# A graph layer's gathers: all but 28 tiles of rows by GpSimd, none picked column by column

## The chip, the core and the metric

The kernel runs on one core of a Trainium2 chip. The core has five engines with a program each: TensorE (PE, matmuls), VectorE (DVE), ScalarE (ACT), GpSimd (POOL) and SyncE (SP, which here issues DMAs). They run side by side and wait for one another through semaphores. The metric is the device time of one execution in microseconds (us), as the median of several runs.

## The reference

One layer of a graph network over 12500 nodes with 128 features and 412500 edges, followed by a layer norm. The edges are sorted by their target `dst`, and `src` is random. Cut to what matters:

```python
f0 = x0 @ W1_0e / sqrt(MUL)                      # node features, x0 = x[:, :32]
f1 = einsum('nui,uw->nwi', x1, W1_1o) / sqrt(MUL)  # x1 = x[:, 32:] as 32 vectors of 3
e0, e1 = feat0[edge_src], feat1[edge_src]        # one row of 128 numbers per edge
h = gelu(gelu(edge_scalar_attr @ W_mlp1 / sqrt(8)) @ W_mlp2 / sqrt(64))
w00, w01, w10, w11 = h @ Wp_00, h @ Wp_01, h @ Wp_10, h @ Wp_11
mid0, mid1 = ...                                 # products of w, e and edge_attr, per edge
n0, n1 = segment_sum(mid0, edge_dst), segment_sum(mid1, edge_dst)
y = cos(MIX) * self + sin(MIX) * (n0 @ W2_0e, n1 @ W2_1o)
out = layernorm(x + y)
```

The step `feat[edge_src]` is the gather that this change is about: 412500 rows of 128 float32 numbers, 512 bytes each, from a table of 12500 rows.

## The kernel before

The edges are cut into runs of 512, 806 of them, the last with 340 edges. A run has four tiles (called columns in the code, q = 0 to 3) of 128 edges, one edge to a partition. Four runs make a chunk, 202 in all. For every run the kernel needs the features of its sources in a buffer `G` of 128 x 4 x 128 numbers. There are LEAD = 19 such buffers.

Before the runs start, a first phase of 25 groups of 512 nodes loads x, transposes it into `xT` (it stays in SBUF, a node to a column), multiplies it by the weights `wf` and stores the result in DRAM as `table`. The first RAW = 18 runs do not wait for the table: their rows of x itself are gathered (indices in `idx_raw`), transposed (`turn_rows`, L569 and L571) and multiplied by `wf` (`features`, L577 and L579), and the result stands in a buffer `ft`; their buffer G is free once it is transposed. All later runs gather finished features from `table`.

Then one long loop goes over the runs s. Its order is written out by hand and holds for PE, ACT, DVE and SP. In iteration s it

- calls `gather(s + 18)`, which takes the next buffer G, the one that run s - 1 had, and so has to wait until that run's reader is done;
- issues some loads of edge data, and 16-row parts of an aided tile (below);
- makes the edge weights of runs ahead on PE (`weights`, L560), and once per chunk the two layers of the small network (`mlp1`, L527 and L531, `mlp2`, L542 and L547);
- sums the messages of run s - 1 on PE (`segments`, L631 and L633), with an address per tile read from a register;
- multiplies weights and features of run s on DVE (`messages`, one product at L602 and two at L606), which frees the buffer G;
- adds a finished chunk into an accumulator (`add`, L646), and about every 32 runs ends a group of nodes (`norm` and what follows it: PE at L662 and L665, ACT at L670, DVE at L678, the store of `out` by SP at L257 and L259).

A tile of rows gets into G in one of three ways:

1. *GpSimd gathers it*: one indirect DMA of 128 rows, L220, with the node numbers in `idx` (transposed by PE for 128 runs at a time).
2. *SyncE copies it* (`aid`, L203 and L207): in every AID = 14th run from run 36 on, the last tile's 128 rows are 128 DMAs of 512 bytes, with node numbers loaded into registers. They are issued in eight sets of 16 rows (ROWS), spread over STEPS = 12 runs, the first 16 runs (AID_LEAD) ahead of use. There are 55 such tiles, 7040 copies.
3. *VectorE or ScalarE picks it* (`pick_nodes` and `pick`): the tile's 128 node numbers, turned into addresses at L163, are loaded into registers (L176), and each node's column is copied out of `xT` into a buffer `gt`, 128 x 1 at a time (DVE at L188, ACT at L190). `picked_rows` then multiplies the finished `gt` by `wf` on PE (L196) and ACT copies the result into G (L197). DVE picks tile q = 2, ACT tile q = 1. The table `SLOTS` says how many columns each picks: DVE 8, 12 and 12 after the three products of a run, ACT 24 or 28 in a run, so a tile takes four or five runs. From the run COL_FROM on this gives 197 tiles of DVE and 157 of ACT.

What the three leave over follows from these lines of `gather`:

```python
            if q == Q - 1 and s in aided or any(q == COL_Q[e] and (e, s) in pick_of for e in picked):
                continue
            rows = idx_raw[:, s, q:q + 1] if s < raw_runs else idx[b][:, q, c:c + 1]
            nc.gpsimd.indirect_dma_start(
```

Of 806 x 4 tiles one lies past the last edge; 3223 - 55 - 354 = 2814 are gathered by GpSimd.

Of the kernel before, what the change touches and what calls it, by code (L numbers as in the profile page):

```python
# [15 lines left out]
ACT = mybir.EngineType.Activation  # L16
DVE = mybir.EngineType.DVE
# [4 lines left out]
P = 128  # L22
# [20 lines left out]
RAW = 18  # L43
MARGIN = 64
ACC = 768
AID = 14
ROWS = 16
AID_FROM = 36
AID_LEAD = 16
STEPS = 12  # L50
SLOTS = {DVE: [(8, 12, 12)], ACT: [(24,), (28,), (24,), (28,), (24,)]}
COL_Q = {DVE: Q - 2, ACT: Q - 3}
COL_FROM = {DVE: 11, ACT: 16}
LNB = 2


# [1 line left out]
def gnn_kernel(ctx: ExitStack, tc: tile.TileContext, x, src, dst, ea4, ea8, w1_0, w1_1, wm1, wm2,  # L58
# [26 lines left out]
    def sub(ap, offset, dims):  # L85
        return bass.AP(tensor=ap.tensor, offset=ap.offset + offset, ap=dims)
# [24 lines left out]
    G, GT, Y = {}, {}, {}  # L111
    aided = range(AID_FROM, NS - 1, AID)

    slot_at = {}
    for e, cycle in SLOTS.items():
        slot_at[e], n = {}, 0
        for s in range(COL_FROM[e], NS):
            for slot, k in enumerate(cycle[(s - COL_FROM[e]) % len(cycle)]):
                slot_at[e][s, slot] = (n, n + k)
                n += k  # L120

    picked = {}
    for e in SLOTS:
        picked[e] = []
# [6 lines left out]
    pick_of = {(e, s): i for e, g in picked.items() for i, s in enumerate(g)}  # L131
    assert AID_FROM >= raw_runs and AID_LEAD < LEAD and P % ROWS == 0 and STEPS <= AID
    assert all(raw_runs <= g[0] and 0 < len(g) <= 3 * P for g in picked.values())
# [5 lines left out]
    def aid_load():  # L139


        nc.sync.dma_start(aid_at, sub(src, AID_FROM * SB + (Q - 1) * P, [[AID * SB, len(aided)], [1, P]]))
        for e, g in picked.items():
            n = sum(sum(run) for run in SLOTS[e])
            cycle, ahead = n // math.gcd(n, P), P // math.gcd(n, P) * len(SLOTS[e])
            assert all(z - a == ahead for a, z in zip(g, g[cycle:]))
# [15 lines left out]
        for rows in pick_tiles:  # L162
            nc.vector.tensor_scalar(rows, rows, 4.0, float(x_at), op0=OP.mult, op1=OP.add)  # L163

    picking = {e: [] for e in picked}

    def pick_nodes(e, s, slot):

        a, z = slot_at[e].get((s, slot), (0, 0))
        z = min(z, P * len(picked[e]))  # L170
        while a < z:
            i, r0 = divmod(a, P)
            r1 = min(P, r0 + z - a)
            if r0 == 0:
                GT[e, i] = wk.tile([P, P], F32, name=f"gt{list(picked).index(e)}", bufs=3)
            _, r = nc.values_load_multi_w_load_instructions(  # L176
                pick_rows[e, i][:, r0:r1], engines=[e], min_val=x_at, max_val=x_at + 4 * (N - 1),
                skip_runtime_bounds_check_because="addresses of columns")
            for k in range(r1 - r0):
                at = r[k].with_bounds(guaranteed_mod_val=0, out_of_modulus=4)  # L180
                picking[e].append((GT[e, i][:, r0 + k:r0 + k + 1], x_bytes[:, bass.ds(at, 4)].bitcast(F32)))
            a += r1 - r0
# [661 lines left out]
    with tc.manual_schedule(engines={PE, ACT, DVE, SP}):  # L844
# [46 lines left out]
        A["now"] = A["next"]  # L891
        clearing = []
        pick_nodes(ACT, 0, 0)
        for s in range(NCH * CH + CH):
            c, k = divmod(s, CH)
# [10 lines left out]
            for t in range(P // ROWS):  # L906
                a = s + AID_LEAD - t * STEPS // (P // ROWS)
                if a in aided:
# [19 lines left out]
            if k > 1 and c + 2 < NCH:  # L928
                pick(ACT, P)
                (mlp1 if k == 2 else mlp2)(c + 2)  # L930
                if k == 3 and c + 3 == NCH:
                    nc.scalar.activation(spent, ones, AF.Sqrt)
            pick(ACT, P)
            pick_nodes(ACT, s + 1, 0)
            if s + 1 < raw_runs:
                turn_rows(s + 1)
            if s < NS:
                for part in range(3):
                    messages(s, part)
                    pick_nodes(DVE, s, part)  # L940
                    pick(DVE, P)
# [53 lines left out]
```

## Time and profile before

| | before |
|---|---|
| runs, us | 3772.66, 3779.92, 3783.14 (median 3779.92) |
| profiled execution, us | 3778.12 |
| its span, first to last instruction, us | 3776.3 |
| mean granted clock of TensorE | 0.903 |
| gathers by GpSimd (from x, from the table) | 72 + 2742 |
| row copies by SyncE | 7040 |
| columns picked by VectorE, by ScalarE | 25216, 20096 |
| DMA, mean over the span | 64 GB/s |

The profile is one execution. Its page gives busy times by engine, the chain of work that ended last followed back from the end, and groups of instructions by line. A group's row reads: line, engine, operation, output and input, shapes and count, then busy time in us and the mean of one in ns, then the idle time of that engine just before these instructions and what ended most of it. "issue" there means that the engine waited for nothing that the profile shows. A row of the timeline reads: start in us, duration in us, engine, line, operation and tiles, and in brackets the idle time ahead of it. The duration of a gather is the time that GpSimd is busy with it, not the time until its rows have landed.

### The profile page before, as it was taken

The numbers are of one execution on the slowest core, as the hardware profiler recorded it, in microseconds if no ns is written. First come the engines' busy times: TensorE is split into PE (matmuls) and PEld (weight loads), VectorE is DVE, ScalarE is ACT, GpSimd is POOL, SyncE is SP. The second block draws the span as 40 slices with busy tenths as digits, with TensorE's granted clock in tenths as the row PEclk, the third lists the DMA queues.
The fourth block names the chain that finished last, engine by engine and source line by source line (L and its number), as shares of the span: only waits on it lengthen the run. The fifth ranks groups of instructions, "written<-read, shape, count | busy, mean of one in ns | idle before, by whom it ended". The sixth has DMA issues, their size and how long they took to land.

```text
span 3776.3 us, 140497 instructions
## 1 busy us (share of the span) xinstructions
PE 3310.0 (88%) x28568; PEld 2904.3 (77%) x28568; DVE 3188.6 (84%) x28801; ACT 2613.7 (69%) x21733; POOL 2678.4 (71%) x2820
## 2 busy tenths in 40 slices
PE   5888898998898999899898898898898889989888
PEld 4777777777777887787777777777787777878777
DVE  3488898888888899888889888888888888988887
ACT  2377677777676777667767677777777777777775
POOL 7667776777777777677777677677777777767770
PEclk8998898998898899889899899999889889889898
DMA  8223222323222223222233223222322222222220
GB/s 203 48 51 67 60 60 62 63 57 70 61 57 63 63 60 68 61 56 63 61 63 68 58 62 63 58 63 62 68 59 60 60 64 62 61 64 62 58 62 14
DMA packets 579364, 240.07 MB, mean 64 GB/s; under 512 B 483702, under 2 KB 528654, under 8 KB 578510
## 3 DMA queue, kind: packets, MB, share of 16 engines
q0 software_dynamic: 90048, 184.60, 19.1%
q1 hardware_dynamic: 467692, 39.95, 8.7%
q10 hardware_dynamic: 20770, 6.47, 0.7%
q8 instruction: 252, 4.13, 0.4%
q14 instruction: 602, 4.93, 0.4%
HBM read 217.98 MB, written 12.80 MB: 61 GB/s over the span
## 4 chain that ended last, share of the span: by engine, by line
DVE 52%; PE 15%; issue 10%; DVEq 7%; SPq 6%; ACT 5%; DMA 3%; POOL 1%; ACTq 0%; POOLq 0%
DVE gt L188 30%; DVE M L606 14%; DVEq L176 7%; SPq L207 4%; DVE M L602 4%; ACT gt L190 3%; PE sums L631 3%; PE sums L633 3%; PE h L665 2%; PE w L560 2%; PE h L527 2%; DMA G<-table,idx 1%; SPq L203 1%; DVE acc L646 1%; POOL G L220 1%
## 5 line engine op out<-in xcount | busy, mean ns | idle before, releaser
L220 POOL DMA_INDIRECT G<-table,idx x2742 | 2609.0, 952 | 988.0 <-issue 759.6
L190 ACT ACTIVATE gt<-xT 128x1 f32 x20096 | 1970.7, 189 | 318.1 <-issue 316.6
L188 DVE COPY gt<-xT 128x1 f32 x25216 | 1758.2, 144 | 306.8 <-issue 210.3
L633 PE MATMUL sums<-own,M 128*128 128x96 f32 x6446 | 1347.3, 293 | 38.0 <-DVE M L606 37.9
L631 PE MATMUL sums<-own,M 128*128 128x96 f32 x6446 | 1379.6, 298 | 0.0
L631 PEld LDWEIGHTS sums<-own,M 128*128 128x128 f32 x6446 | 1078.5, 207 | 84.4 <-issue 18.7
L633 PEld LDWEIGHTS sums<-own,M 128*128 128x128 f32 x6446 | 1069.5, 208 | 51.6 <-DVE M L606 50.8
L560 PE MATMUL w<-wpb,h 64*128 64x128 f32 x6448 | 722.8, 311 | 269.2 <-DVE M L606 268.2
L560 PEld LDWEIGHTS w<-wpb,h 64*128 64x128 f32 x6448 | 545.6, 201 | 426.9 <-DVE M L606 308.9
L606 DVE TENSOR_TENSOR M<-w,G 128x384 f32<-128x384 f32 x1576 | 861.5, 547 | 0.0
L531 ACT ACTIVATE h<-h 128x512 f32<-128x512 f32 x404 | 216.7, 587 | 226.2 <-PE h L527 215.6
L527 PE MATMUL h<-eT,w1b 64*128 64x128 f32 x3232 | 328.9, 349 | 10.1 <-ACT G L197 7.3
L602 DVE TENSOR_TENSOR M<-w,G 128x256 f32<-128x256 f32 x788 | 321.9, 409 | 10.0 <-ACT G L197 4.0
L527 PEld LDWEIGHTS h<-eT,w1b 64*128 64x128 f32 x3232 | 281.1, 246 | 41.2 <-issue 16.8
L542 PE MATMUL h<-h,w2b 64*64 64x256 f32 x3232 | 248.1, 392 | 3.1 <-ACT h L531 2.6
L197 ACT ACTIVATE G<-h 128x128 f32<-128x128 f32 x354 | 96.2, 272 | 209.0 <-PE h L196 186.8
L547 ACT ACTIVATE h<-h 128x512 f32<-128x512 f32 x404 | 214.4, 580 | 29.5 <-PE h L542 24.3
L196 PE MATMUL h<-wf,gt 128*128 128x128 f32 x708 | 152.0, 298 | 17.1 <-ACT eT L520 14.9
L542 PEld LDWEIGHTS h<-h,w2b 64*64 64x64 f32 x3232 | 117.0, 133 | 62.7 <-ACT G L197 9.9
L595 DVE TENSOR_TENSOR own<-oh,e 128x512 f32<-128x512 f32 x202 | 140.3, 695 | 7.1
L196 PEld LDWEIGHTS h<-wf,gt 128*128 128x128 f32 x708 | 114.0, 203 | 25.2 <-ACT eT L520 23.5
L646 DVE TENSOR_TENSOR acc<-sums,acc 128x384 f32 x202 | 111.1, 550 | 8.5 <-issue 6.2
(112 smaller groups left out, 1232.9 us busy)
## 6 DMA issues: line engine op xcount, KB each, us to landing
G<-table SPq DMA_DIRECT2D x7040, 0.5 KB
G<-table,idx POOLq DMA_INDIRECT x2742
e<-in_edge_attr SPq DMA_DIRECT2D x201, 64.0 KB
xt<-in_x SPq DMA_DIRECT2D x24, 256.0 KB
table<-ft ACTq DMA_DIRECT2D x24, 256.0 KB
xt<-in_edge_attr SPq DMA_DIRECT2D x24, 256.0 KB
out<-y SPq DMA_DIRECT2D x24, 256.0 KB
xt<-in_dst SPq DMA_DIRECT2D x5, 256.0 KB
```

Source lines behind the costliest of these rows:

```text
L176: _, r = nc.values_load_multi_w_load_instructions(pick_rows[e, i][:, r0:r1], engines=[e], min_val=x_at, max_val=x_at + 4 * (N - 1), skip_r ...
L188: nc.vector.tensor_copy(to, col)
L190: nc.scalar.activation(to, col, AF.Copy)
L196: nc.tensor.matmul(pt, GT.pop((e, i)), wf, start=True, stop=True)
L220: nc.gpsimd.indirect_dma_start(out=G[s][:, q, :], out_offset=None, in_=x if s < raw_runs else table, in_offset=bass.IndirectOffsetOnAxis(a ...
L527: nc.tensor.matmul(p1[h][:, j // 2, j % 2, :], w1b[rows, j, :], eT[c][rows, :], start=True, stop=True)
L542: nc.tensor.matmul(p2[r][k * HID:(k + 1) * HID, h * n:(h + 1) * n], w2b[rows, :], H1[c][h][rows, k * n:(k + 1) * n], start=True, stop=True)
L560: nc.tensor.matmul(WP[i][:, q, :], H2[c][q % 2][rows, k, q // 2, :], wpb[rows, :], start=True, stop=True)
L602: nc.vector.tensor_tensor(M[s][:, :, :, :MUL], w[:, :, :2 * MUL].rearrange("p q (a u) -> p q a u", a=2), g[:, :, None, :MUL].to_broadcast( ...
L606: nc.vector.tensor_tensor(M[s][:, :, j, MUL:].rearrange("p q (i u) -> p q i u", i=3), w[:, :, None, (2 + j) * MUL:(3 + j) * MUL].to_broadc ...
L631: nc.tensor.matmul(flat[:, bass.ds(at, 4 * FIRST_HALF)].bitcast(F32), M[s][:, q, 0, :], own[:, 3 * WIDE:], start=False, stop=False)
L633: nc.tensor.matmul(sb[:, 1:, bass.ds(at, 4 * WIDE)].bitcast(F32), M[s][:, q, 1, :], own[:, :3 * WIDE].rearrange("p (a j) -> p a j", a=3), ...
```

## The change

The table of picked columns becomes empty, the aided run is every 28th, and its row copies are spread over 16 runs. The rest of the diff lets the loop run with an empty table; `COL_FROM` has no effect then.

```diff
-AID = 14
+AID = 28
 ROWS = 16
 AID_FROM = 36
 AID_LEAD = 16
-STEPS = 12
-SLOTS = {DVE: [(8, 12, 12)], ACT: [(24,), (28,), (24,), (28,), (24,)]}
+STEPS = 16
+SLOTS = {}
 COL_Q = {DVE: Q - 2, ACT: Q - 3}
-COL_FROM = {DVE: 11, ACT: 16}
+COL_FROM = {DVE: 7, ACT: 16}
...
-    picking = {e: [] for e in picked}
+    picking = {e: [] for e in (DVE, ACT)}
...
-        a, z = slot_at[e].get((s, slot), (0, 0))
-        z = min(z, P * len(picked[e]))
+        a, z = slot_at[e].get((s, slot), (0, 0)) if e in picked else (0, 0)
+        z = min(z, P * len(picked.get(e, ())))
```

With the table empty, `picked` has no entries: L163, L176, L188, L190, L196 and L197 are not in the program, and no pick tables are loaded. The aided tiles are 28 (runs 36, 64 and so on to 792), 3584 row copies. GpSimd's list has 3195 gathers. With 16 steps the eight sets of an aided tile stand 16, 14, 12 and so on to 2 runs ahead of its use; with 12 steps the last stood 6 ahead.

## The prediction

> **What bounds the kernel now.** First the page: busy time by engine, and the chain of waits by engine.
>
> ```profile
> PE 3310.0 (88%) x28568; PEld 2904.3 (77%) x28568; DVE 3188.6 (84%) x28801; ACT 2613.7 (69%) x21733; POOL 2678.4 (71%) x2820
> DVE 52%; PE 15%; issue 10%; DVEq 7%; SPq 6%; ACT 5%; DMA 3%; POOL 1%; ACTq 0%; POOLq 0%
> ```
>
> By these two lines VectorE (DVE) and TensorE (PE) set the pace, GpSimd (POOL) has 29% to spare and stands in 1% of the chain. So work taken from VectorE and given to GpSimd looks like a gain. The next view, the groups of instructions, contradicts the spare time.
>
> ```profile
> L220 POOL DMA_INDIRECT G<-table,idx x2742 | 2609.0, 952 | 988.0 <-issue 759.6
> L190 ACT ACTIVATE gt<-xT 128x1 f32 x20096 | 1970.7, 189 | 318.1 <-issue 316.6
> L188 DVE COPY gt<-xT 128x1 f32 x25216 | 1758.2, 144 | 306.8 <-issue 210.3
> ...
> L197 ACT ACTIVATE G<-h 128x128 f32<-128x128 f32 x354 | 96.2, 272 | 209.0 <-PE h L196 186.8
> ...
> L196 PE MATMUL h<-wf,gt 128*128 128x128 f32 x708 | 152.0, 298 | 17.1 <-ACT eT L520 14.9
> ```
>
> Of GpSimd's 988 us idle ahead of its gathers, 759.6 are put down to "issue", that is, to nothing else on the chip. The timeline of GpSimd alone shows what that is. Its columns: start, duration, instruction, and in brackets the idle time before it.
>
> ```profile
> 5.00 0.94 POOL L220 DMA_INDIRECT G<-in_x,idx_raw  x1 [0.30 <-issue]
> ...
> 52.43 0.94 POOL L220 DMA_INDIRECT G<-in_x,idx_raw  x1 [0.30 <-issue]
> ...
> 2000.14 0.94 POOL L220 DMA_INDIRECT G<-table,idx  x1 [0.30 <-DMA G<-table]
> 2001.39 0.94 POOL L220 DMA_INDIRECT G<-table,idx  x1 [0.30 <-issue]
> ...
> 2058.82 0.94 POOL L220 DMA_INDIRECT G<-table,idx  x1 [0.30 <-DMA G<-table]
> ```
>
> From 5.00 to 52.43 there are 38 steps from one start to the next, from 2000.14 to 2058.82 there are 47: 1.248 us a step in both. Each gather is 0.94 us busy and 0.30 us of fixed idle time that no wait explains. GpSimd is a metronome: it can start a gather every 1.25 us and no faster, and its "71% busy" is close to its ceiling. The last view says how close, counting the gathers of the long steady stretch:
>
> ```profile
> 211.00:3691.00 3480.00, 2543.91 (x2674) 0.90 0.29 62
> ```
>
> This row of the windows (stretch, length, busy time and count of the gathers, granted clock, DMA share, GB/s) has 2674 gathers in 3480 us, 1.301 us each. With the mean duration of 0.952 us and 0.305 us of fixed idle time (1.2485 less the median 0.944, in the row under the rivals) a free-running GpSimd takes 1.257 us a gather: the 0.952 holds the occasional longer ones. So GpSimd already runs at 97% of its free rate; the rest is waiting for G buffers. What is bound today is the whole machine at once: GpSimd, VectorE and TensorE were balanced by the picked columns.
>
> **The change part by part.** *Removed from VectorE and ScalarE:* 25216 copies (1758.2 us) and 20096 (1970.7 us), the 354 tile multiplications (708 matmuls, 152.0 us) and 354 evictions (96.2 us). What remains is DVE 3188.6 - 1758.2 = 1430, ACT 2613.7 - 1970.7 - 96.2 = 547, PE 3310.0 - 152.0 = 3158 us. None of the three can be the bound at 3900 us or more. The loads of the pick tables and their address arithmetic go as well, all on engines that now have slack; I book nothing for them.
>
> *Added to GpSimd:* 806 runs of 4 tiles less one tile past the last edge are 3223. Before, 55 come from SyncE's row copies and 354 are picked, which leaves 2814 gathers (2742 and 72 in the rows). After, every 28th run from run 36 gives 28 aided tiles and none are picked: 3223 - 28 = 3195 gathers, 381 more. At 1.257 us that is 479 us. Its floor, 3195 x 1.257 = 4016 us, is above the whole present span of 3776.3 us. This is the result in short; the rest is where the ends lie.
>
> *The start.* Gathers of runs 0 to 36 are issued while the first 18 runs, computed from raw rows of x, are processed at the pace of PE and ACT; the 19 G buffers are then the limit. Run 37 takes the buffer of run 18, so it starts when the last message product of run 18 is done:
>
> ```profile
> 174.05 0.42 DVE L602 TENSOR_TENSOR M<-w,ft 128x256 f32<-128x256 f32 x1 [0.99 <-ACT ft L579]
> ...
> 179.10 0.42 DVE L602 TENSOR_TENSOR M<-w,ft 128x256 f32<-128x256 f32 x1 [0.99 <-ACT ft L579]
> ...
> 194.33 0.42 DVE L602 TENSOR_TENSOR M<-w,ft 128x256 f32<-128x256 f32 x1 [3.31 <-ACT ft L579]
> ...
> 201.87 0.42 DVE L602 TENSOR_TENSOR M<-w,ft 128x256 f32<-128x256 f32 x1 [3.49 <-ACT ft L579]
> ...
> 206.72 0.58 DVE L188 COPY gt<-xT 128x1 f32 x8
> ...
> 207.92 0.82 DVE L188 COPY gt<-xT 128x1 f32 x12 [0.16 <-issue]
> 208.66 0.55 DVE L606 TENSOR_TENSOR M<-w,G 128x384 f32<-128x384 f32 x1
> ```
>
> Before, run 37 starts at 209.97, with 8.27 us of waiting:
>
> ```profile
> 199.40 0.60 ACT L571 ACTIVATE xt<-h 128x512 f32<-128x512 f32 x1 [0.79 <-ACT gt L190]
> ...
> 209.97 0.94 POOL L220 DMA_INDIRECT G<-table,idx  x1 [8.27 <-ACT h L531]
> ```
>
> Without the copies run 18 loses the 0.58 + 0.82 us between its products. The step from 194.33 to 201.87, 7.5 us, contains ScalarE's first copies (one eviction waits for them, row of 199.40); the like step from 174.05 to 179.10 took 5.05, so I take off 2.5. Together 3.9: run 37 starts at 206. The bounds: 188 (no hold-up at all: 3.6 + 147 x 1.257, since 147 gathers precede it after the change) and 210 (nothing gained).
>
> *The long middle.* From run 37 on 3195 - 147 = 3048 gathers remain, 3047 steps to the last start: 3830 us at 1.257. Does GpSimd wait for buffers on this way? Message products of table runs start as follows (count, shortest/median/longest ns, first and last start):
>
> ```profile
> L602 DVE TENSOR_TENSOR M<-w,G x788: 351/414/425, 206.2 to 3760.3; 128x256 f32<-128x256 f32 x197
> ```
>
> 787 steps in 3554 us: even with all copies the other engines take 4.52 us a run. GpSimd will need 3048/769 x 1.257 = 4.98. So they empty its 18-run lead, at 0.46 us a run or faster, and from then on everyone waits for GpSimd and buffers are always free. The lead of 18 x 4.98 = 90 us lasts 195 runs at most; the present waiting, 3480 - 2674 x 1.257 = 119 us over 787 runs, would cost 29 us in these if it stayed. I take 0, because without copies the lead shrinks from the first run and a shrunken lead covers the hold-ups; 29 is the upper end.
>
> *SyncE.* Its row copies halve and are spread over 16 runs, not 12, the last 16 rows being programmed two runs ahead of use.
>
> ```profile
> L207 SPq DMA_DIRECT2D G<-table x7040: 227/228/378, 198.0 to 3694.2; - x196
> ```
>
> Sixteen of them take about 4 us, less than one run's 4.98; should a set be late behind an output store, the consumers wait, not GpSimd. That costs nothing while they are faster, and the last aided run, 792, is 13 runs from the end. Cover gone, one late set would cost some 5 us.
>
> On these rows the page Perfetto Trace Analysis of the Trainium skill (section DMA Optimizations) speaks against the change: where descriptor generation is the bottleneck, DMAs should be balanced over the engines that can issue them. The trace agrees in price: the 27 tiles that go from SyncE back to GpSimd are 27 x 1.257 = 34 us of the 479.
>
> *The end.* Now the last gather starts 86 us ahead of the end, since GpSimd runs ahead; afterwards it is last. Behind it stand its landing and what follows the last run's products:
>
> ```profile
> 278.63 2.48 DMA G<-table,idx
> ...
> 3690.14 0.94 POOL L220 DMA_INDIRECT G<-table,idx  x1 [0.30 <-issue]
> ...
> 3760.33 0.36 DVE L602 TENSOR_TENSOR M<-w,G 128x256 f32<-128x256 f32 x1
> ```
>
> The chain gives 2.48 us from a gather's start to its landing, and from 3760.33 to the span's end at 3776.3 are 16.0 us (sums, the last layer norm, the store). I book 18.5.
>
> *Sum:* 206 + 3830 + 18.5 = 4054.5 us of span. The profiled execution took 3778.12 for a span of 3776.3, so 1.8 lie around it: **4056 us**. That execution is 1.8 below the median of the runs, 3779.92. Check by differences: 3778 + 479 (gathers) - 119 (waits of the steady stretch) - 67 (86 to 18.5 at the end) - 14 (the hold-up at the start was 209.97 - 3.6 - 139 x 1.257 = 31.7 and is 206 - 188.4 = 17.6) = 4057.
>
> **The rivals.** *A, faster: the chain of waits is right.* If VectorE's copies set the end, the time falls towards TensorE: 3158 us at today's 88% share is 3590. GpSimd would have to start a gather every (3590 - 40)/3195 = 1.11 us; the point from which the change gains at all is (3778 - 40)/3195 = 1.17. Here is every gather of the trace, with shortest, median and longest duration in ns, and the reach of the copies:
>
> ```profile
> L220 POOL DMA_INDIRECT G<-table,idx x2742: 938/944/1475, 94.4 to 3690.1; - x196
> L220 POOL DMA_INDIRECT G<-in_x,idx_raw x72: 940/944/1375, 3.6 to 93.1; - x72
> L188 DVE COPY gt<-xT x25216: 130/144/157, 162.8 to 3735.3; 128x1 f32 x199
> ```
>
> None is under 0.938 us, and the 0.30 us between them never shrank. I give A 3%.
>
> *B: the copies slow the gathers,* which become shorter without them. For it speak the longer gathers that lift the mean to 952. Against it: before 162.8 us there are no copies, and the median is the same 944 ns, with 1375 as the longest. Were all 3195 as short as the shortest, 0.938 + 0.305, the sum falls by 14 ns x 3048 = 43 to 4013. I give it 5%. The Trainium skill's SBUF — State Buffer (section Who interferes with whom) has the rule behind it: VectorE copies in a two-port mode lock GpSimd out of the shared ports, where it writes descriptors. By that rule the gathers should be longer while 25216 copies run; the trace disagrees, 944 ns on either side of 162.8 us.
>
> *C: the waits for buffers stay,* and GpSimd keeps its present 1.301 us a gather: 206 + 3047 x 1.301 + 20.3 = 4190. For it: these waits name message products, evictions and PE, of which most remain. Against it: they need a full lead, and 4.52 against 4.98 us a run empties it. 5%.
>
> *D: the change does not do what it says,* and some tiles do not reach GpSimd. The changed program's list has 3195 gathers and no L188 or L190; below 1%.
>
> **How the numbers follow.** My own case has 86%. Its spread: the start -18 to +4, the middle -43 to +29, the end some 2 either way; these do not all fall together, so 4025 to 4085 holds it, and with it most of the 8 in 10. A measurement of this kernel tells about 0.3%, 11 us, from no change. Faster: A, 0.03. Within 0.3%: 0.01. Slower: all else, 0.96.
>
> **What would show it.** Right: 3195 gathers at a step of 1.25 us from run 37 to the last, nearly all idle time before them "issue", GpSimd at some 75% of the span and the last gather 18 to 20 us before its end; VectorE near 1430 us, waiting for gathers in every run. Wrong: steps under 1.2 us (A or B), waits on message products late in the span (C), or gathers that end well before the span does.

## The result, and the profile after

| | before | after |
|---|---|---|
| median, us | 3781.18 (4 runs, 3772.66 to 3783.14) | 4035.53 (4 runs, 4034.90 to 4037.28) |
| ratio, 95% interval | | 1.0678 (1.0660 to 1.0697) |
| profiled execution, its span, us | 3778.12, 3776.3 | 4037.28, 4035.5 |
| gathers by GpSimd | 72 + 2742 | 72 + 3123 |

The kernel became 6.8% slower. The forecast was 4056, in a range of 4025 to 4085. The page's engine line, its chain of waits and the first of its groups, for the changed kernel:

```profile
PE 3399.6 (84%) x27860; PEld 2969.8 (74%) x27860; DVE 1525.3 (38%) x3581; ACT 658.7 (16%) x1283; POOL 3028.9 (75%) x3201
POOL 47%; issue 31%; PE 11%; DMA 7%; DVE 2%; SPq 1%; ACT 1%; POOLq 0%; DVEq 0%; ACTq 0%
L220 POOL DMA_INDIRECT G<-table,idx x3123 | 2960.0, 948 | 962.6 <-issue 913.0
L602 DVE TENSOR_TENSOR M<-w,G 128x256 f32<-128x256 f32 x788 | 332.9, 422 | 2281.2 <-DMA G<-table,idx 2003.0
```

GpSimd is only 75% busy, four points more than before. But the chain of waits now runs through its gathers (47%) and through the "issue" time between them (31%), where before it had 1% and 10%. VectorE's busy time is halved, and in place of copies it has 2281 us of idle time ahead of the first product of a run, 2003 of them ended by a gather's landing. One row of the windows and three of GpSimd's timeline give the pace and the start (window: stretch, length, busy time and count of the gathers, clock, DMA share, GB/s):

```profile
199.30:4015.00 3815.70, 2887.05 (x3047) 0.85 0.28 61
```

```profile
199.34 0.94 POOL L220 DMA_INDIRECT G<-table,idx  x1 [1.75 <-DVE M L606]
200.59 0.94 POOL L220 DMA_INDIRECT G<-table,idx  x1 [0.30 <-issue]
201.83 0.94 POOL L220 DMA_INDIRECT G<-table,idx  x1 [0.30 <-issue]
```

From the first gather of run 37 at 199.34 there is not one wait for a buffer any more: 3047 steps in 3816 us, 1.2524 us each. The table of GpSimd's waits says the same for the whole span; its columns are total us, times, and the longest one:

```profile
POOL G L220 <- issue: 934.3, 3064, 0.6
POOL G L220 <- DMA G<-table,idx: 21.4, 70, 0.3
POOL G L220 <- PE h L569: 11.6, 9, 2.2
POOL G L220 <- DVE M L606: 6.3, 16, 1.7
```

The kernel before had this row for the message products (L606):

```profile
POOL G L220 <- DVE M L606: 111.6, 125, 6.7
```

The waits of 0.3 us are the fixed idle time under another name.

### The profile page after: what moved, and what is told of

It is laid out like the page before. It is cut to its first block, busy times and chain, and to the rows that moved or that the text cites. A ratio compares the mean times of both kernels' runs of the same rounds, so it can differ in the third digit from the quotient of the medians.

```text
span 4035.5 us, 82434 instructions
## 1 busy us (share of the span) xinstructions
PE 3399.6 (84%) x27860; PEld 2969.8 (74%) x27860; DVE 1525.3 (38%) x3581; ACT 658.7 (16%) x1283; POOL 3028.9 (75%) x3201
## 4 chain that ended last, share of the span: by engine, by line
POOL 47%; issue 31%; PE 11%; DMA 7%; DVE 2%; SPq 1%; ACT 1%; POOLq 0%; DVEq 0%; ACTq 0%
POOL G L220 47%; DMA G<-table,idx 6%; PE sums L631 3%; PE sums L633 2%; PE w L560 2%; DMA xt<-in_x 1%; PE h L665 1%; PE h L527 1%; PE h L542 1%; SPq L207 1%; DVE M L606 1%; PE h L577 1%; PE h L662 0%; DVE M L602 0%; ACT xt L571 0%
## 5 line engine op out<-in xcount | busy, mean ns | idle before, releaser
L220 POOL DMA_INDIRECT G<-table,idx x3123 | 2960.0, 948 | 962.6 <-issue 913.0
L631 PE MATMUL sums<-own,M 128*128 128x96 f32 x6446 | 1467.9, 314 | 73.9 <-DVE M L606 73.4
L633 PE MATMUL sums<-own,M 128*128 128x96 f32 x6446 | 1423.6, 307 | 0.2
L631 PEld LDWEIGHTS sums<-own,M 128*128 128x128 f32 x6446 | 1144.6, 220 | 190.3 <-DVE M L606 103.0
L633 PEld LDWEIGHTS sums<-own,M 128*128 128x128 f32 x6446 | 1141.3, 221 | 20.0 <-DVE M L606 19.2
L560 PE MATMUL w<-wpb,h 64*128 64x128 f32 x6448 | 754.2, 326 | 456.1 <-DVE M L606 456.0
L606 DVE TENSOR_TENSOR M<-w,G 128x384 f32<-128x384 f32 x1576 | 797.5, 548 | 0.0
L595 DVE TENSOR_TENSOR own<-oh,e 128x512 f32<-128x512 f32 x202 | 139.6, 691 | 8.3
L520 ACT ACTIVATE eT<-h 128x128 f32<-128x128 f32 x202 | 56.0, 277 | 495.0 <-PE h L518 490.7
L665 PE MATMUL h<-wpost,acc 128*128 128x128 f32 (+1 forms) x784 | 104.2, 277 | 0.0
L665 PEld LDWEIGHTS h<-wpost,acc 128*128 128x128 f32 (+1 forms) x784 | 96.1, 193 | 0.0
L220 POOL DMA_INDIRECT G<-in_x,idx_raw x72 | 68.4, 950 | 24.2 <-issue 21.3
L625 PE MATMUL sums<-none 128*128 128x480 bf16 x202 | 80.5, 398 | 0.0
```

The costliest lines, as they stand in the source:

```text
L220: nc.gpsimd.indirect_dma_start(out=G[s][:, q, :], out_offset=None, in_=x if s < raw_runs else table, in_offset=bass.IndirectOffsetOnAxis(a ...
L560: nc.tensor.matmul(WP[i][:, q, :], H2[c][q % 2][rows, k, q // 2, :], wpb[rows, :], start=True, stop=True)
L595: nc.vector.tensor_tensor(to, hot[:, :, None, :].to_broadcast([P, n * Q, 4, J]), a[:, :, :, None].to_broadcast([P, n * Q, 4, J]), op=OP.mult)
L606: nc.vector.tensor_tensor(M[s][:, :, j, MUL:].rearrange("p q (i u) -> p q i u", i=3), w[:, :, None, (2 + j) * MUL:(3 + j) * MUL].to_broadc ...
L631: nc.tensor.matmul(flat[:, bass.ds(at, 4 * FIRST_HALF)].bitcast(F32), M[s][:, q, 0, :], own[:, 3 * WIDE:], start=False, stop=False)
L633: nc.tensor.matmul(sb[:, 1:, bass.ds(at, 4 * WIDE)].bitcast(F32), M[s][:, q, 1, :], own[:, :3 * WIDE].rearrange("p (a j) -> p a j", a=3), ...
```

## The experiments

All of e1 to e11 start from the changed kernel, e12 from the one before. The median of the kernel before, run beside them, was between 3772 and 3778.

**e1, SyncE's tiles back.**

```diff
-AID = 28
+AID = 14
-STEPS = 16
+STEPS = 12
```

> The changed kernel with the aided run every 14th again and its copies over 12 runs (55 tiles by SyncE, none picked): 3168 gathers, 27 fewer. Theory (GpSimd's step is the bound, 1.2525 us a gather in the changed kernel's trace): 4035.5 - 27 x 1.2525 = 4002, between 3996 and 4008. Rival (the copies picked by VectorE and ScalarE alone mattered, SyncE's tiles are hidden either way): no change, 4030 to 4041. Rival (SyncE's 7040 row copies slow the gathers, as longer ones were more frequent before): 4010 to 4020, mean gather back near 952 ns.

Measured: 4002.9 (4000.82 to 4007.09), 1 us from the theory. 27 gathers fewer are 32.6 us less, 1.21 us each, so neither rival holds. SyncE's 3456 additional copies did not lengthen the gathers: their mean is 947 ns.

**e2 and e3, one picker back.**

```diff
-SLOTS = {}
-COL_FROM = {DVE: 7, ACT: 16}
+SLOTS = {ACT: [(24,), (28,), (24,), (28,), (24,)]}   # e2
+SLOTS = {DVE: [(8, 12, 12)]}                         # e3
+COL_FROM = {DVE: 11, ACT: 16}
```

> The changed kernel with ScalarE's picking put back (157 tiles), VectorE's not, SyncE at 28 tiles: 3038 gathers. Theory: 4035.5 - 157 x 1.2525 = 3839, between 3830 and 3850, GpSimd's idle time still nearly all issue. Rival (the four engines share the bound once ScalarE is loaded again): above 3860, with waits of GpSimd for message products late in the span.

> The changed kernel with VectorE's picking put back (197 tiles), ScalarE's not: 2998 gathers. Theory: 4035.5 - 197 x 1.2525 = 3789, between 3780 and 3805, if the other engines keep a pace under 4.67 us a run (2998 gathers' share), which VectorE with its copies did before (4.52 with both sets of copies). Rival (VectorE's copies bind by themselves): above 3810, and GpSimd waits for message products to the end.

Measured: e2 3846.6 (3844.92 to 3848.64), 8 above the theory's point and within its range; e3 3821.0 (3819.30 to 3823.24), 32 above it: outside the theory's range, and by its number in the rival's. The gathers' groups, of e2 first and then of e3, show half of why:

```profile
L220 POOL DMA_INDIRECT G<-table,idx x2966 | 2809.5, 947 | 922.4 <-issue 824.2
```

```profile
L220 POOL DMA_INDIRECT G<-table,idx x2926 | 2791.3, 954 | 914.6 <-issue 792.1
```

In both kernels the last gather starts 19 us ahead of the end of the span (3824.9 of 3843.9, 3798.7 of 3817.5), so GpSimd is the bound in both. The rival for e3 asked for waits on message products to the end. GpSimd's table of waits in e3 has them 120 times, 0.3 us each, the fixed idle time:

```profile
POOL G L220 <- DVE M L606: 37.0, 120, 0.7
```

So VectorE did not bind. But with its copies a gather takes 954 ns on average, not 948, which is some 18 us over the 2850 gathers that follow the start; the rest lies at the start, where GpSimd's last wait for a buffer ends at 204.7 us in place of 199.3. Gathers that are longer beside VectorE's copies are what rival B of the prediction spoke of, here at a small scale; e5, e6 and e10 look into it.

**e4, half of the gather left to SyncE with other rows.**

```diff
+            if s >= raw_runs and q < 2:
+                nc.sync.dma_start(G[s][:, q, :], table[s * 14:s * 14 + P, :])
+                continue
```

> The changed kernel with the first two tiles of every run from run 18 on loaded by one SyncE DMA each of 128 consecutive table rows, so the rows are those of other nodes: it leaves out half of the gather. 1619 gathers by GpSimd, whose floor falls to some 2050 us. It shows the pace of all other engines without any picked column. Theory: GpSimd alone held them at 4.98 us a run, so the time falls to what TensorE allows, 3400 to 3650 (rival A of the prediction priced that at 3590). Rival (TensorE or the order of the loop binds without the copies too): above 3900.

Measured: 3445.6, one run. With GpSimd relieved, the same loop without a picked column runs 590 us faster. So TensorE, VectorE and ScalarE were not what held the changed kernel. 3446 is an upper end for their own pace, since SyncE's loads were late in places. VectorE's waits for rows that SyncE loads, in this run:

```profile
DVE M L605 <- DMA G<-table: 632.3, 35, 28.1
```

**e5, e6 and e10, copies for nothing.** All tiles are gathered, and VectorE works beside them. In e5 it copies columns as before the change, in e6 each copy is a reduction, in e10 the copies read fixed columns.

```diff
+SLOTS = {DVE: [(8, 12, 12)]}
...
-            if q == Q - 1 and s in aided or any(q == COL_Q[e] and (e, s) in pick_of for e in picked):
+            if q == Q - 1 and s in aided:
...
-        nc.tensor.matmul(pt, GT.pop((e, i)), wf, start=True, stop=True)
-        nc.scalar.activation(G[picked[e][i]][:, COL_Q[e], :], pt, AF.Copy)
+        GT.pop((e, i))
...
-                nc.vector.tensor_copy(to, col)
+                nc.vector.tensor_reduce(to, col, axis=mybir.AxisListType.X, op=OP.add)   # e6
...
+                picking[e].append((GT[e, i][:, r0 + k:r0 + k + 1], xT[:, 89 * k:89 * k + 1]))   # e10, no register loads
```

> The changed kernel, all 3195 gathers kept, with VectorE's 25216 column copies of before beside them, whose result nobody reads. Theory (the copies lengthen some gathers, as the mean of 954 ns with VectorE's picking against 948 without and 947 with ScalarE's suggests): 4035.5 + 3047 x 0.0065 + some 8 at the start, 4055 to 4070, gather mean 953 to 955 ns. Rival (the copies leave the gathers alone, and 954 came from the picked tiles' waits): 4034 to 4044, mean 948.

> As e5, but each idle copy of a column is a reduction over its one element: the same count of VectorE instructions with the same reads, writes and register addresses, in an operation that has no two-port mode by the Trainium skill's SBUF — State Buffer. If the two-port mode of copies lengthens the gathers: mean back to 947 to 948 ns, 4036 to 4046. If it is the number of VectorE instructions, their fetching or their SBUF traffic: as e5, mean 953 to 955 and the same time within 6 us.

> As e5, but the 25216 idle copies read fixed columns, so that the register loads ahead of them (2364 in the trace of before, about 0.85 us each) are gone. If these loads lengthen the gathers: gather mean back to 948 ns, 4035 to 4045. If it is the copies or the fetching of so many instructions: mean 953 to 955, 4050 to 4065.

Measured: e5 4061.4 (4060.03 to 4063.97), as the theory has it; e6 4060.7 (4058.08 to 4062.92), its second case; e10 4066.9 (4061.72 to 4068.89), 2 above its second case. The gathers' groups of e5, e6 and e10 in this order:

```profile
L218 POOL DMA_INDIRECT G<-table,idx x3123 | 2978.0, 954 | 967.0 <-issue 817.5
```

```profile
L218 POOL DMA_INDIRECT G<-table,idx x3123 | 2976.3, 953 | 967.1 <-issue 809.4
```

```profile
L214 POOL DMA_INDIRECT G<-table,idx x3123 | 2989.6, 957 | 965.6 <-issue 867.6
```

25216 small VectorE instructions that nobody needs cost 25 to 31 us, with gathers that are 5 to 9 ns longer on average and a somewhat later start. Neither the kind of operation nor the register loads matter: the reductions and the fixed columns do no less. With ScalarE's 20096 copies the mean stayed at 947 ns (e2).

The mean hides that only a few gathers grow, and the traces show which. Once per chunk VectorE runs the product at L595 (it writes `own` from `oh` and `e`, 0.69 us). A gather that starts while it runs ends, in most cases, about 0.82 us after it. First the changed kernel, then e5, where the line is L593:

```profile
3614.52 0.69 DVE L595 TENSOR_TENSOR own<-oh,e 128x512 f32<-128x512 f32 x1
3614.59 1.44 POOL L220 DMA_INDIRECT G<-table,idx  x1 [0.30 <-issue]
```

```profile
1822.81 0.69 DVE L593 TENSOR_TENSOR own<-oh,e 128x512 f32<-128x512 f32 x1
1822.96 1.35 POOL L218 DMA_INDIRECT G<-table,idx  x1 [0.30 <-issue]
```

Counted over all gathers of a trace:

| kernel | gathers over 0.96 us | of these, beside that product | mean of all others, ns |
|---|---|---|---|
| before | 102 | 94 | 944 |
| changed | 65 | 59 | 944 |
| e2, ScalarE's copies | 48 | 38 | 944 |
| e3, VectorE's copies | 131 | 126 | 944 |
| e4, no copies, half of the gathers | 177 | 173 | 943 |
| e5, e6, e10, copies for nothing | 142, 134, 113 | 136, 132, 108 | 944 |

So it is not the copies beside a gather that lengthen it (in e5 2758 of 3195 gathers have copies beside them), but this product, and with VectorE's copies, reductions or copies from fixed places more gathers meet it. The gathers over 0.96 us hold 31.9 us beyond 0.944 each in e5 and 13.5 in the changed kernel; that and the start of run 37 (204.0 for 199.3) make up e5's loss. That the copies act by shifting the product against the gathers is an argument: no run moved the product alone. e4 fits it, with the most long gathers and no copy at all. It is not the two-port mode that the Trainium skill's SBUF — State Buffer (section Who interferes with whom) holds responsible, as by that page a reduction never takes the shared ports.

**e9, the SyncE part of the change alone.**

```diff
-SLOTS = {}
+SLOTS = {DVE: [(8, 12, 12)], ACT: [(24,), (28,), (24,), (28,), (24,)]}
-COL_FROM = {DVE: 7, ACT: 16}
+COL_FROM = {DVE: 11, ACT: 16}
```

> The change's SyncE part alone: both pickers as before, the aided run every 28th with its copies over 16 runs, 2841 gathers, 27 more than before. Theory: the kernel before waits 119 us for buffers in its steady stretch, so 27 x 1.257 = 34 us of gathers go into waits that are there anyway: within 20 us of before, 3765 to 3800. Rival (the full 34 us show, as GpSimd had no slack): 3805 to 3820.

Measured: 3765.5, ratio to before 0.9970 (0.9955 to 0.9985). The 27 more gathers cost nothing while the pickers work: GpSimd's waits for message products fell from 111.6 to 71.5 us, and the slack took them. Why the kernel is even 0.3% faster was not looked into; SyncE had half of its copies. So the loss comes from emptying the table of picked columns. SyncE's part costs something only once the table is empty and GpSimd has no waits left: the same 27 tiles are 32.6 us in e1.

**e7, e8 and e11, other mixes.** If the count of gathers sets the time until the other engines bind, a split that loads VectorE less should beat the kernel before.

```diff
-AID = 28
-STEPS = 16
-SLOTS = {}
-COL_FROM = {DVE: 7, ACT: 16}
+AID = 14                                        # e7, e11; e8: 11
+STEPS = 12                                      # e7, e11; e8: 11
+SLOTS = {DVE: [(0, 0, 20)], ACT: [(28,)]}       # e7, e8; e11: 24 in place of 20
+COL_FROM = {DVE: 11, ACT: 16}
```

> A mix that follows from e1 to e4: SyncE 55 tiles, ScalarE 28 columns a run, VectorE 20 a run and all behind the last product; 2874 gathers. Theory (GpSimd's count sets the time while the others keep 4.45 us a run): 4035.5 - 321 x 1.2525 = 3633, with up to 20 for longer gathers and the start 3633 to 3660. Rival (with three pickers loaded, no engine is the bound alone and the loop's waits add up as in the kernel before): 3720 to 3790, GpSimd waiting for message products to the end.

> As e7 with SyncE at 70 tiles (every 11th run): 2859 gathers. Theory: 15 x 1.2525 = 19 us below e7. Rival (waits): no faster than e7, or slower because SyncE's in-order queue is late.

> As e7 with 24 columns a run by VectorE in place of 20: 25 tiles more picked, 2849 gathers. Theory: GpSimd still the bound, 25 x 1.2525 = 31 us below e7's 3670: 3635 to 3650. Rival (the others' pace binds now): 3660 to 3700, and waits of GpSimd for message products grow.

Measured: e7 3669.8 (3668.23 to 3672.41), ratio 0.9713 (0.9683 to 0.9743), the fastest of the kernels here that gather every row; e8 4153.9; e11 3752.3 (3733.75 to 3755.65), ratio 0.9924 (0.9895 to 0.9954). All three missed the theory's range: e7 by 10, the other two by much, e8 as its rival said and e11 even above its rival's. First and last gather of e7 and of e11 (count, shortest, median and longest ns, first and last start):

```profile
L220 POOL DMA_INDIRECT G<-table,idx x2802: 939/944/1457, 93.8 to 3650.7; - x187
```

```profile
L220 POOL DMA_INDIRECT G<-table,idx x2777: 938/944/1465, 94.4 to 3672.0; - x199
```

In e7 the last gather stands 17 us ahead of the end of its span (3667.7), and none waits for a buffer after 211 us: GpSimd binds to the last. In e11 it stands 78 us ahead (3750.5): the other engines fall behind, and with 25 gathers saved the kernel takes 82 us more. The chains of e7 and e11, in this order:

```profile
ACT 31%; PE 24%; issue 14%; POOL 11%; SPq 8%; DMA 7%; ACTq 2%; DVE 2%; DVEq 1%; POOLq 0%
```

```profile
ACT 41%; PE 28%; issue 11%; POOL 5%; DMA 4%; SPq 4%; DVE 3%; ACTq 2%; DVEq 1%; POOLq 0%
```

In e11 ScalarE and TensorE have grown in it, VectorE hardly. Why four columns more on VectorE cost that much was not found. In e8 the third supplier gave out. SyncE's own timeline of e8 (start, duration, instructions):

```profile
2000.96 5.13 SPq L207 DMA_DIRECT2D G<-table  x16
...
2009.47 12.13 SPq L207 DMA_DIRECT2D G<-table  x32
2021.70 0.40 SPq L487 DMA_DIRECT2D e<-in_edge_attr  x1
2023.53 11.66 SPq L207 DMA_DIRECT2D G<-table  x32
2035.29 0.40 SPq L487 DMA_DIRECT2D e<-in_edge_attr  x1
2037.59 18.16 SPq L207 DMA_DIRECT2D G<-table  x48
```

From 2009.47 to 2023.53 are 14.06 us for two sets of 16 rows and one load of edge data of 0.40: 6.8 us a set with its register load. 70 tiles of eight sets are 560 sets, some 3800 us, in a stretch of 3898 (first and last start of the copies, after count and shortest, median and longest ns):

```profile
L207 SPq DMA_DIRECT2D G<-table x8960: 227/228/403, 199.9 to 4098.3; - x200
```

So SyncE is full, and the loads of edge data behind them in the same queue come late. TensorE's wait in e8 names them:

```profile
PE h L518 <- DMA e<-in_edge_attr: 386.5, 105, 7.6
```

**e12, the place of VectorE's copies.**

```diff
-SLOTS = {DVE: [(8, 12, 12)], ACT: [(24,), (28,), (24,), (28,), (24,)]}
+SLOTS = {DVE: [(0, 0, 32)], ACT: [(24,), (28,), (24,), (28,), (24,)]}
```

> The kernel before with VectorE's 32 columns a run all behind the last product instead of 8, 12 and 12 behind each; counts unchanged, 2814 gathers. If the place is what made e7 faster: 3590 to 3680, GpSimd's waits for message products mostly gone. If it is the number of columns (20 for 32): as before within 1%, 3740 to 3810.

Measured: 3730.1 (3724.36 to 3737.40), ratio 0.9890 (0.9871 to 0.9910), between the two. Putting the copies behind the last product gains 1.1%, of the 2.9% of e7; GpSimd still waits for message products (68.2 us in 107 waits). The rest of e7's gain goes with its other counts, which were not tried one by one.

## Why the prediction was right, by its steps

**The bound.** That GpSimd's 71% was near its ceiling, one gather in 1.25 us however much the other engines have to do, is shown. The median step is 1.249 us before and after, and the time goes with the count of gathers in kernels whose other loads differ widely: e1, e2 and e3 lie 1, 8 and 32 us above 4035.5 less 1.2525 a gather. The engine line and the chain of waits of the kernel before would have misled. Its chain gave GpSimd 1%, probably because GpSimd ran ahead: its last gather stands 86 us before the end. The chain misleads in e7 too, where GpSimd binds and has 11%.

**The sum**, term by term, in us:

| term | forecast | measured | off by |
|---|---|---|---|
| first gather of run 37 | 206 | 199.3 | -6.7 |
| 3047 steps to the last gather | 3830 | 3816.1 | -13.9 |
| last gather's start to the end | 18.5 | 20.0 | +1.5 |
| span | 4054.5 | 4035.5 | -19.0 |

*The start* was mis-sized. Run 18's products on VectorE's timeline of the changed kernel:

```profile
184.52 0.42 DVE L602 TENSOR_TENSOR M<-w,ft 128x256 f32<-128x256 f32 x1 [5.12 <-ACT ft L579]
...
191.41 0.42 DVE L602 TENSOR_TENSOR M<-w,ft 128x256 f32<-128x256 f32 x1 [4.61 <-ACT ft L579]
...
196.46 0.42 DVE L602 TENSOR_TENSOR M<-w,ft 128x256 f32<-128x256 f32 x1 [3.70 <-ACT ft L579]
...
197.73 0.41 DVE L602 TENSOR_TENSOR M<-w,G 128x256 f32<-128x256 f32 x1
198.06 1.01 DVE L606 TENSOR_TENSOR M<-w,G 128x384 f32<-128x384 f32 x2
```

The prediction took 2.5 us off one step and 1.4 off run 18. Both came (the step from 191.41 to 196.46 is the foreseen 5.05), but run 17's own copies went too: from its first product to run 18's are 1.27 us where 201.87 to 206.18 had 4.31. And the step ahead took 6.9 us, not the 8.3 of 186.04 to 194.33 that was left as it stood, and began 1.5 us earlier.

*The middle* was priced with the mean gather of before, 952 ns. It is 948 without VectorE's copies. That is what rival B foresaw, put aside because the median before and after the first copy is the same. The median was the wrong row for this question, since only a few gathers grow: the mean shows it (952 and 948 ns), and neither the median (944 in both) nor the longest does (1475 and 1506). e5 gives the price, 26 us, start included. B's effect came beside the main one, of a size within its bound of 43, but not by B's mechanism: the long gathers are those that meet the product at L595.

*The waits for buffers* were taken to vanish, and did: rival C falls. The lead was empty early, as computed from 4.52 against 4.98 us a run: from run 73 on, at 385 us, VectorE waits for a gather's landing in most runs (627 of 733), where up to 195 runs were allowed for. In VectorE's timeline:

```profile
385.30 0.42 DVE L602 TENSOR_TENSOR M<-w,G 128x256 f32<-128x256 f32 x1 [1.88 <-DMA G<-table,idx]
...
390.40 0.42 DVE L602 TENSOR_TENSOR M<-w,G 128x256 f32<-128x256 f32 x1 [3.75 <-DMA G<-table,idx]
...
395.51 0.42 DVE L602 TENSOR_TENSOR M<-w,G 128x256 f32<-128x256 f32 x1 [3.29 <-DMA G<-table,idx]
```

*The end* is 2.80 us of landing and 17.2 behind it, where 2.5 and 16.0 were booked.

**Rival A** fell by e4 together with the result. Its price for a machine with no bound on gathers was 144 us too high: 3590 against 3446. What failed was its condition, a gather in 1.11 us, which no kernel here shows.

**SyncE** was called free, and in this change it is: e1 gives 1.21 us a tile, the price of GpSimd's gather and nothing more. But its cost was mis-sized. Sixteen copies take 5.1 us and 6.8 with the register load, not 4: the median of 228 ns leaves out what lies between two copies. At 28 tiles this is hidden, at 70 it sets the time (e8).

**What remains of the other engines** was too low for all three: VectorE 1525 us for 1430, ScalarE 659 for 547, TensorE 3400 for 3158. Rows of the timeline overlap (the copies at 207.92 last 0.82 us, the next product starts at 208.66), so a group's busy time cannot simply be subtracted; for TensorE see the last section. It had no effect on the time.

## What to carry to other kernels

An engine that issues transfers back to back, with a fixed pause in each, is full at a busy share well under 100% (here 75%). Take the distance from start to start in an undisturbed stretch and multiply it by the count: that floor, not the busy share or the chain of waits, says what it can still take on. A tile that three engines can supply is worth splitting until their floors are even (e7), and not past it (e8, e11). Work that an engine does on the way to freeing a buffer belongs behind the step that frees it (1.1% in e12).

## What the runs showed of the hardware that had not been expected

A gather that starts while VectorE runs the product at L595 ends, in most cases, 0.82 us after that product, so it takes up to some 1.46 us in place of 0.94 (e5: 125 of 150 such gathers are over 0.96 us). Nearly all others take 0.94 us, with VectorE's small instructions beside them or without. TensorE, which now waits more (84% busy for 88%), was granted a mean clock of 0.856 where it had 0.903, and its matmuls were longer. The group of L631, which had 298 ns before:

```profile
L631 PE MATMUL sums<-own,M 128*128 128x96 f32 x6446 | 1467.9, 314 | 73.9 <-DVE M L606 73.4
```

314 to 298 is the ratio of the two clocks, 1.05. So TensorE's busy time rose to 3399.6 us though it had 708 matmuls fewer; the clock alone would make 3158 some 3330, and the rest is open. That the waiting lowered the clock was not tested.
